# Two graph-attention layers on one core: other places for the mask preparation and the prologue, symmetry check and two normalizations on ScalarE

## The chip, the core and the metric

The kernel runs on one core of a Trainium2 chip. A core has TensorE (matrix products, written as PE), VectorE (DVE), ScalarE (ACT), GpSimd (POOL) and SyncE (SP), which here issues nearly all DMAs. The engines run side by side and wait for each other by semaphores; each works off its own instructions in the order in which the program issues them. The metric is the time of the whole program on the device in microseconds (us), lower is better.

## The reference

x is 16 batches of 1024 rows by 256 features; adj is a symmetric 0/1 matrix of 1024 x 1024 per batch with ones on the diagonal. Two layers are computed, each on relu(layernorm(x)) and each added to x:

```python
h = maximum(layernorm(x), 0)
x = x + L0(h, adj, ...)          # attention with 8 heads of 32, then an MLP
h = maximum(layernorm(x), 0)
x = x + L1(h, adj, ...)          # graph attention with one head

def L0(x, adj):
    qkv = heads(layer_norm(x) * gamma1 + beta1)       # queries = keys = values
    attn = softmax(where(adj > 0, qkv @ qkv.T / sqrt(32), -inf))
    x = x + attn @ qkv
    y = layer_norm(x) * gamma2 + beta2
    return x + gelu(y @ W1 + b1) @ W2 + b2

def L1(f, adj):
    h = f @ W
    e = leaky_relu((h @ a_1).T + h @ a_2 + h @ a_12 @ h.T, 0.2)
    p = softmax(where(adj > 0, e, -9e15))
    return elu(f @ W_1 + (p @ f) @ W_2)
```

## The kernel before

`fast_path` treats the 16 batches in two parts that overlap: while TensorE works on the attention of batch b (`attention`, the first half of the first layer), it also works on what remains of batch b-1 (`rest`: MLP and second layer). A third piece, `prologue`, loads the x of batch b+1 and prepares its h, values va and transposed keys kT meanwhile. Nothing is looped at run time; all instructions are written out.

**The order.** Generators (`stream_a` for the attention, `stream_b` for rest, `stream_p`, `stream_c` for the prologue, `stream_m` for the masks, `stream_k` for the symmetry check, `stream_s`) each hand out a place, a number in which batch b's attention runs from b to b+1. The one with the lowest place issues its next piece. `spread(pieces, n, start, end)` gives n pieces equal distances. So a change of start and end moves a piece's instructions in every queue that it uses. Besides, `defer(us, f)` puts f off until an estimate of the time issued so far, `clock`, has gone on by us; `run_deferred` issues what is due. At the end the program order is fixed for every engine.

**Attention.** A unit is one tile of 128 keys against 512 queries for 4 heads: scores on TensorE (L994), mask added by VectorE (L1007), exponential with row sum by ScalarE (L1014), and one unit later the product with the values (L1109). Batch 0 has 32 units and lets TensorE add half of the masks. From batch 1 on there are 24: since the scores are symmetric, the exponentials of 8 units of the first query half are turned by VectorE (L1030), written to HBM (blocks), and read back for the second half (em, L1077, used by L1091). GpSimd sums up the turned tiles (part, L1043).

**rest.** For four groups c of 256 rows: `prepare` measures mean and variance (`norm_stats`, whose power of -0.5 is on GpSimd, L746) and 5 us later normalizes on VectorE (`normalize`, L750) into y; `turn` transposes y (pty) and applies gamma2 and beta2 (yT); `expand` and `contract` are the MLP (ph, hid, po). `prepare1` and `turn1` do the same for the second layer (ft, ptf, and fT with a relu on ScalarE). Then come the projection uT (copied out of PSUM by ScalarE, L1364), the values gw (by ScalarE and VectorE in turn, L1379), the logits lg with mask and leaky relu on VectorE (L1397, L1402), their exponential (L1403), pf and pa (z and en, L1418 to L1450), and the store. PSUM has three tiles (psm) for all of these but scores and sums.

**prologue.** For four groups: load h, measure, rectify (L803: ScalarE's relu with a scale and a bias nm from VectorE, L798), measure again, values va (L750, L816, L817), transposition ptk and its copy kT (L827). Its 28 pieces lie between b-0.70 and b-0.25.

**Masks.** `turn_masks(b, qh)` loads four row tiles of adj as two halves each (adjp has two buffers), converts them on VectorE to fp8 (mq, L594; `mqp` has one buffer) and turns them by DMA transposes into mk (L904; `mkp` has four). `compare_masks` subtracts, on GpSimd, mk from mq in a block of 128x512 (odd, L919), which is all zeros if adj is symmetric, and VectorE ORs the result into uneven (L926) 3 us later. At the end uneven's largest byte goes into seen, and the program repeats the work on a general path if it isn't 0.

**Buffers.** tmpp holds tags w1 (six buffers: nrm, z, en), w2 (five: os, the copied sums, and ot), y (y and ft) and yT.

```python
            else:
                yield from spread(prologue(b, states[b]), 28, b - 0.700, b - 0.250)
    def stream_m():
        for b in range(B):
            if b:
                yield from spread(turn_masks(b, 0, states[b]), 5, b - 0.17, b - 0.01)
            start = b + (0.36 if b else 0.23)
            yield from spread(turn_masks(b, 1, states[b]), 5, start, start + 0.2)
    def stream_k():
        for b in range(B):
            yield from spread(compare_masks(b, 0, states[b]), TPH, b + 0.02, b + 0.2)
            yield from spread(compare_masks(b, 1, states[b]), 2 * TPH, b + (0.58 if b else 0.52), b + 0.73)
```

Of the kernel before, what the change touches and what calls it, by code (L numbers as in the profile page):

```python
# [9 lines left out]
F32 = mybir.dt.float32  # L10
BF16 = mybir.dt.bfloat16
# [484 lines left out]
def fast_path(  # L496
# [47 lines left out]
    xbp = pool("xbp", NT)  # L544
    adjp = pool("adjp", 2)
    mqp = pool("mqp", 1)
    mkp = pool("mkp", 4)
    hp = pool("hp", 2)
    vp = pool("vp", 2)
    midp = pool("midp", 1)  # L550
# [106 lines left out]

    seen = const.tile([P, 6], F32, name="seen")
    nc.gpsimd.memset(seen[:, 5:6], 0.0)
    uneven = const.tile([P, QW // 2], I32, name="uneven")  # L660
    nc.gpsimd.memset(uneven, 0)

# [70 lines left out]
    def norm_stats(srcs, name):  # L735

        nt = len(srcs)
        st = smallp.tile([P, nt, nc.vector.BN_STATS_DIM], F32, tag="st", name=f"st_{name}")
        mv = smallp.tile([P, nt, nc.vector.BN_AGGR_DIM], F32, tag="mv", name=f"mv_{name}")
        for t in range(nt):  # L740
            nc.vector.bn_stats(st[:, t, :], srcs[t])
            nc.vector.bn_aggr(mv[:, t, :], st[:, t, :])
        ve = smallp.tile([P, nt], F32, tag="ve", name=f"ve_{name}")
        nc.vector.tensor_scalar_add(ve, mv[:, :, 1], EPS)
        rs = smallp.tile([P, nt], F32, tag="rs", name=f"rs_{name}")
        nc.gpsimd.tensor_tensor(rs, ve, mhalf[:, :nt], op=ALU.pow)  # L746
        return mv, rs

    def normalize(dst, src, mv, rs, t):
        nc.vector.tensor_scalar(  # L750
            dst, src, mv[:, t, 0:1], rs[:, t : t + 1], op0=ALU.subtract, op1=ALU.mult
        )

    clock = [0.0]
    deferred = []

    def defer(us, f):
        deferred.append((clock[0] + us, len(deferred), f))  # L760

        return clock[0] + us
# [148 lines left out]
    def compare_masks(b, qh, st):  # L911

        for half in range(qh + 1):
            for i in range(TPH):
                kt = qh * TPH + i
                odd = smallp.tile([P, QW], BF16, tag="odd", bufs=2, name=f"odd_{b}_{qh}_{half}_{i}")
                key = st[half][:, kt // 2, :, kt % 2]
                query = st["mq", qh][:, i, half * QW : (half + 1) * QW]
                nc.gpsimd.tensor_tensor(  # L919
                    odd.rearrange("p (u v x) -> p u v x", u=2, v=2),  # L920
                    key.rearrange("p (u v x) -> p u v x", u=2, v=2),
                    query.rearrange("p (u x v) -> p u v x", u=2, v=2),
                    op=ALU.subtract,
                )
                o = odd.bitcast(I32)
                defer(3.0, lambda o=o: nc.vector.tensor_tensor(uneven, uneven, o, op=ALU.bitwise_or))  # L926
                yield
        if (b, qh) == (B - 1, NQH - 1):
            defer(
                4.0,  # L930
                lambda: nc.vector.tensor_reduce(
                    seen[:, 4:5], uneven.bitcast(U8), axis=mybir.AxisListType.X, op=ALU.max
                ),
            )

# [17 lines left out]
    def finish(b, qh, g, rl, ready, os):  # L953
        h = hs[b]
        run_deferred(ready)
        finished[b, qh] = finished.get((b, qh), 0) + 1
        clock[0] += 0.5
        pt = ps_tile([P, TPH, P], f"ptos_{b}_{g}_{qh}")
        for t in range(TPH):
            nc.tensor.transpose(pt[:, t, :], os[:, t * P : (t + 1) * P], ident)  # L960
        ot = tmpp.tile([P, TPH, GH, HD], F32, tag="w2", bufs=5, name=f"ot_{b}_{g}_{qh}")
        nc.vector.tensor_mul(  # L962
            ot, pt.rearrange("p t (j d) -> p t j d", d=HD), rl.unsqueeze(3).to_broadcast([P, TPH, GH, HD])
        )
        ho = h[qh][:, :, g * P : (g + 1) * P]
        nc.gpsimd.tensor_add(ho, ho, ot.rearrange("p t j d -> p t (j d)"))  # L966

    def attention(b, st):
# [135 lines left out]
        def weigh(qh, g, kt, es, first, last):  # L1104
            if first and not (mirrored and qh == 1):
                acc[g, qh] = pso.tile([P, QW], F32, tag="o", name=f"o_{b}_{g}_{qh}")
            o = acc[g, qh]
            for j in range(GH):
                nc.tensor.matmul(  # L1109
                    o[j * HD : (j + 1) * HD, :],  # L1110
                    va[:, kt, (g * GH + j) * HD : (g * GH + j + 1) * HD],
                    es[j // 2][:, j % 2, :],
                    start=first and not (mirrored and qh == 1),
                    stop=last,
                )
            if last:
                c = os[g, qh] = tmpp.tile([P, QW], F32, tag="w2", bufs=5, name=f"os_{b}_{g}_{qh}")
                nc.vector.tensor_copy(c, o)
                if qh == NQH - 1:
                    close(qh, g)  # L1120
# [89 lines left out]
    def prepare(b, st, c):  # L1210

        h = hs[b]
        assert finished[b, c // 2] == NG
        ts = range(c * TPC, (c + 1) * TPC)
        mv, rs = norm_stats([h[t // TPH][:, t % TPH, :] for t in ts], f"c{b}_{c}")

        def apply():
            y = tmpp.tile([P, TPC, D], F32, tag="y", name=f"y_{b}_{c}")
            for i, t in enumerate(ts):
                normalize(y[:, i, :], h[t // TPH][:, t % TPH, :], mv, rs, i)  # L1220
            st["y", c] = y, None

        st["y", c] = None, defer(5.0, apply)

    def count_fit(lo, hi, i):

# [5 lines left out]
    def rest(b, st, tails):  # L1232
# [30 lines left out]
                yield 0.0, None  # L1263

        def turn(c):
            if st["y", c][1] is not None:
                run_deferred(st["y", c][1])
            y = st["y", c][0]
            for i in range(TPC):
                defer(4.0 * i + 2.0, lambda t=c * TPC + i: add_residuals(t))  # L1270
            yT[c] = tmpp.tile([P, DC, CW], F32, tag="yT", name=f"yT_{b}_{c}")
            pt = ps_tile([P, DC, CW], f"pty_{b}_{c}")
            for dc in range(DC):
                for i in range(TPC):
                    nc.tensor.transpose(
                        pt[:, dc, i * P : (i + 1) * P], y[:, i, dc * P : (dc + 1) * P], ident
                    )
            for dc in range(DC):
                nc.vector.tensor_scalar(  # L1279
                    yT[c][:, dc, :],  # L1280
                    pt[:, dc, :],
                    g2[:, dc : dc + 1],
                    be2[:, dc : dc + 1],
                    op0=ALU.mult,
                    op1=ALU.add,
                )
# [44 lines left out]
        ft, ready1 = {}, {}  # L1331

        def prepare1(c):
            mv, rs = norm_stats(xt[c * TPC : (c + 1) * TPC], f"d{b}_{c}")

            def apply():
                ft[c] = tmpp.tile([P, TPC, D], F32, tag="y", name=f"ft_{b}_{c}")
                for i in range(TPC):
                    normalize(ft[c][:, i, :], xt[c * TPC + i], mv, rs, i)

            ready1[c] = defer(5.0, apply)

        def turn1(c):
            run_deferred(ready1[c])
            fT = st["fT"]
            pt = ps_tile([P, DC, CW], f"ptf_{b}_{c}")
            for i in range(TPC):
                for dc in range(DC):
                    nc.tensor.transpose(
                        pt[:, dc, i * P : (i + 1) * P], ft[c][:, i, dc * P : (dc + 1) * P], ident  # L1350
                    )
            nc.scalar.activation(fT[:, :, c * CW : (c + 1) * CW], pt, AF.Relu)

        def project(qh, oc, fT, uT):
            pp = ps_tile([P, QW], f"puT_{b}_{oc}_{qh}")
# [249 lines left out]
    def stream_c():  # L1605
        for b in range(B):
            if b == 0:
                yield -0.6
                for place, _ in zip((0.02, 0.04, 0.07, 0.10, 0.13), prologue(b, states[b])):
                    yield place  # L1610
            else:
                yield from spread(prologue(b, states[b]), 28, b - 0.700, b - 0.250)

    def stream_m():
        for b in range(B):
            if b:
                yield from spread(turn_masks(b, 0, states[b]), 5, b - 0.17, b - 0.01)
            start = b + (0.36 if b else 0.23)
            yield from spread(turn_masks(b, 1, states[b]), 5, start, start + 0.2)

    def stream_k():
        for b in range(B):
            yield from spread(compare_masks(b, 0, states[b]), TPH, b + 0.02, b + 0.2)
            yield from spread(compare_masks(b, 1, states[b]), 2 * TPH, b + (0.58 if b else 0.52), b + 0.73)

    def stream_s():
        yield -0.3
# [3 lines left out]
        for i, _ in enumerate(check_products()):  # L1631
            yield 1.32 + 0.03 * i

    streams = [stream_s(), stream_a(), stream_b(), stream_p(), stream_c(), stream_m(), stream_k()]
    places = [next(s, None) for s in streams]
    while any(p is not None for p in places):
        i = min((p, i) for i, p in enumerate(places) if p is not None)[1]
# [72 lines left out]
```

## Time and profile before

| | us |
|---|---|
| median of 3 runs | 3430.3 (3427.79 to 3435.07) |
| the profiled execution | 3435.34 |
| its span, first to last instruction | 3433.2 |
| granted TensorE clock in it, share of full speed | 0.993 |

The profile is of one execution. Busy time of an engine is the union of its instructions' times. Batches 2 to 14 take 207 to 215 us each, from the first scores of one to those of the next (the first scores of batch 4 start at 769.4 us, those of batch 5 at 979.5); after 3280 us only the last batch's rest is left. A time named with a position, such as 874.12, counts from the start of the span; the ones named in what follows lie in batch 4's attention or just behind it. A wait is put down to the instruction whose semaphore came last.

The costliest groups (line, engine, operation, output and inputs, shapes, count; busy us, mean ns; idle before):

```profile
L1014 ACT ACTIVATE e<-e 128x512 f32<-128x512 f32 x1504 | 928.5, 619 | 839.7 <-DVE e L1007 837.5
L1007 DVE TENSOR_TENSOR e<-s,mk 128x1024 f32<-128x1024 f32 x752 | 885.1, 1216 | 204.1 <-PE s L994 197.5
```

### The profile page before, as it was taken

Reading aid. Unit: us, or ns where it says so; the run is one execution under the profiler, and the core shown is the slowest. Engines: PE = TensorE matmul, PEld = TensorE weight load, DVE = VectorE, ACT = ScalarE, POOL = GpSimd, SP = SyncE. Lnnn points to the kernel's source line nnn. Section 1 sums busy time; section 2 is a strip of 40 time slices with the busy share of each in tenths; the row PEclk is TensorE's granted clock in tenths of the full one; section 3 lists DMA queues with packets and bytes.
Section 4 is the critical chain, followed back from the end, with each engine's and each line's share of the span. In section 5 each row is a group of like instructions: output and inputs, shape, how many; then the busy total and the mean of one; then the engine's idle time right before and its main releaser. Section 6 shows DMA issues by size and latency. Waiting matters only on the chain. (4 is left out here: it accounts for less than half of the span.)

```text
span 3433.2 us, 114690 instructions
## 1 busy us (share of the span) xinstructions
PE 3239.3 (94%) x48866; PEld 1590.8 (46%) x48866; DVE 2791.5 (81%) x5201; ACT 1966.2 (57%) x4744; POOL 1535.2 (45%) x1758
## 2 busy tenths in 40 slices
PE   6899999999999999999999999999999999999998
PEld 1344444444444444444444444444444444444477
DVE  6788888888888888887888888888888888887844
ACT  6765745647456474655646556475564745646442
POOL 3553553535535254462545526355353554525220
PEclk9999999999999999999999999999999999999999
DMA  5245455464555545555454555545546445554510
GB/s 134 58 115 157 94 121 125 114 158 99 133 121 122 140 109 121 127 120 144 113 134 112 122 138 119 139 109 125 126 113 158 99 121 132 116 143 101 132 38 14
DMA packets 741158, 404.81 MB, mean 118 GB/s; under 512 B 173216, under 2 KB 699936, under 8 KB 740640
## 3 DMA queue, kind: packets, MB, share of 16 engines
q1 hardware_dynamic: 740352, 397.14, 47.9%
q8 instruction: 386, 6.32, 0.8%
q14 instruction: 132, 1.08, 0.1%
q10 hardware_dynamic: 288, 0.26, 0.0%
HBM read 233.97 MB, written 146.54 MB: 111 GB/s over the span
## 5 line engine op out<-in xcount | busy, mean ns | idle before, releaser
L1014 ACT ACTIVATE e<-e 128x512 f32<-128x512 f32 x1504 | 928.5, 619 | 839.7 <-DVE e L1007 837.5
L1007 DVE TENSOR_TENSOR e<-s,mk 128x1024 f32<-128x1024 f32 x752 | 885.1, 1216 | 204.1 <-PE s L994 197.5
L574 PE MATMUL ph<-yT,w 128*32 128x256 f32 x7808 | 445.8, 379 | 16.4 <-DVE yT L1279 15.0
L574 PE MATMUL pa<-gw,e 128*32 128x258 f32 x7584 | 446.4, 380 | 9.1 <-DVE e L1397 9.1
L574 PE MATMUL lg<-fT,uT 128*32 128x256 f32 x7680 | 452.3, 380 | 0.0
L994 PE MATMUL s<-kT 32*64 32x512 f32 x6272 | 447.0, 622 | 1.1 <-DVE e L1007 1.1
L574 PE MATMUL po<-w,hid 128*32 128x256 f32 x7680 | 434.4, 379 | 0.0
L1109 PE MATMUL o<-e,va 128*32 128x512 f32 x3136 | 428.8, 614 | 1.4 <-ACT e L1014 1.4
L574 PEld LDWEIGHTS ph<-yT,w 128*32 128x32 f32 x7808 | 250.4, 110 | 220.2 <-DVE yT L1279 32.5
L574 PEld LDWEIGHTS po<-w,hid 128*32 128x32 f32 x7680 | 250.0, 110 | 202.7 <-issue 48.5
L574 PEld LDWEIGHTS lg<-fT,uT 128*32 128x32 f32 x7680 | 248.5, 110 | 200.2 <-issue 29.7
L574 PEld LDWEIGHTS pa<-gw,e 128*32 128x32 f32 x7584 | 247.5, 110 | 196.0 <-issue 22.1
L1043 POOL TENSOR_TENSOR part<-part,x 128x512 f32<-128x512 f32 x240 | 309.3, 1289 | 18.8
L1030 DVE STREAM_TRANSPOSE x<-e 128x1024 f32<-128x1024 f32 x240 | 291.5, 1232 | 9.9 <-ACT e L1014 8.2
L966 POOL TENSOR_TENSOR h<-h,ot 128x512 f32<-128x512 f32 x64 | 82.1, 1282 | 455.3 <-DVE ot L962 455.3
L1397 DVE SCALAR_TENSOR_TENSOR e<-lg,gw,mk 128x256 f32<-128x256 f32 x512 | 222.9, 476 | 72.3 <-PE lg L574 62.3
L1014 ACT ACTIVATION_READ_ACCUMULATOR e<-e 128x1 f32 x1504 | 281.1, 187 | 0.0
L1403 ACT ACTIVATE e<-e,shift 128x512 f32<-128x512 f32 x256 | 183.1, 716 | 150.8 <-DVE e L1402 141.1
L1303 ACT ACTIVATE hid<-ph,b1c 128x256 f32<-128x256 f32 x512 | 203.6, 465 | 83.7 <-PE ph L574 61.3
L1043 POOL TENSOR_TENSOR part<-x 128x512 f32<-128x512 f32 x120 | 155.3, 1294 | 208.6 <-DVE x L1030 151.2
L919 POOL TENSOR_TENSOR odd<-mk,mq 128x512 bf16<-128x512 fp8e5 x192 | 236.2, 1237 | 20.9 <-DVE uneven L926 18.7
L1109 PEld LDWEIGHTS o<-e,va 128*32 128x32 f32 x3136 | 63.2, 108 | 327.4 <-issue 212.8
(143 smaller groups left out, 4380.4 us busy)
## 6 DMA issues: line engine op xcount, KB each, us to landing
blocks<-x SPq DMA_DIRECT2D x480, 256.0 KB, 4.7
em<-blocks SPq DMA_DIRECT2D x240, 512.0 KB, 5.0
adj<-in_adj_dram SPq DMA_DIRECT2D x248, 256.0 KB, 4.1
h<-in_x_dram SPq DMA_DIRECT2D x64, 256.0 KB, 4.2
xb<-in_x_dram SPq DMA_DIRECT2D x128, 128.0 KB, 3.4
out_dram<-z SPq DMA_DIRECT2D x128, 128.0 KB, 4.1
rows<-row SPq DMA_DIRECT2D x120, 32.0 KB, 2.6
gather<-rows SPq DMA_DIRECT2D x120, 32.0 KB, 3.3
```

Of the source, the lines that this page charges most:

```text
L574: nc.tensor.matmul(out[c : c + HD], lhsT[:, c : c + HD], rhs, start=start, stop=stop)
L919: nc.gpsimd.tensor_tensor(odd.rearrange("p (u v x) -> p u v x", u=2, v=2), key.rearrange("p (u v x) -> p u v x", u=2, v=2), query.rearrang ...
L966: nc.gpsimd.tensor_add(ho, ho, ot.rearrange("p t j d -> p t (j d)"))
L994: nc.tensor.matmul(sc[j // 2][c : c + P // 2, j % 2, :], kT[r, g, kt * P + c : kt * P + c + P // 2], kT[r, g, qs], start=j >= by_pe, stop= ...
L1007: nc.vector.tensor_tensor(e, masked, mb, op=ALU.add)
L1014: nc.scalar.activation(e[:, j], masked[:, j], AF.Exp, scale=SCALE, accum_out=sums[kt // TPH, g][:, n, kt % TPH, qh : qh + 1],)
L1030: nc.vector.transpose(x[:, :, 2 * i : 2 * i + 2, :].rearrange("p c h j -> p h c j"), es[i].rearrange("p h (c i) -> p h c i", i=HD),)
L1043: add = lambda out, p, q: nc.gpsimd.tensor_tensor(out, p, q, op=ALU.add)
L1109: nc.tensor.matmul(o[j * HD : (j + 1) * HD, :], va[:, kt, (g * GH + j) * HD : (g * GH + j + 1) * HD], es[j // 2][:, j % 2, :], start=first ...
L1303: nc.scalar.activation(hid[:, f0 + i, :], ph[:, i, :], AF.Identity, bias=b1c[:, f0 + i : f0 + i + 1])
L1397: nc.vector.scalar_tensor_tensor(e[:, j, :], lg[:, j, :], gw[:, kt, D : D + 1], st[c // 2][:, kt // 2, qs, kt % 2], op0=ALU.add, op1=ALU.add,)
L1403: ready = defer(2.5, lambda: nc.scalar.activation(e, e, AF.Exp, bias=shift))
```

## The change

It has four parts. (1) The prologue's pieces lie between b-0.60 and b-0.15. (2) The masks: turn_masks of the first half goes from b-0.17..b-0.01 to b-0.43..b-0.25 (batch 1: b-0.28..b-0.10), and of the second half, from batch 1 on, from b+0.36..b+0.56 to b+0.03..b+0.20; the comparisons follow each; `mkp` gets a fifth buffer, w2 gives one up. (3) The symmetry check: odd lies in a w1 buffer, and instead of VectorE's OR ScalarE squares it and adds up the row into a column of uneven; at the end the columns are added. (4) y and ft are normalized by ScalarE with a scale and a bias, as the rectify is; the bias nm2 is a small VectorE instruction 3 us after the statistics, and ft's relu is part of it, so that fT is a plain copy.

```diff
-    mkp = pool("mkp", 4)
+    mkp = pool("mkp", 5)
-    uneven = const.tile([P, QW // 2], I32, name="uneven")
-    nc.gpsimd.memset(uneven, 0)
+    uneven = const.tile([P, B * 3 * TPH], F32, name="uneven")
+    def normalize_later(dst, srcs, stats, name, function):
+        mv, rs = stats
+        nm = smallp.tile([P, TPC], F32, tag="nm2", name=f"nm_{name}")
+        defer(
+            3.0, lambda: nc.vector.scalar_tensor_tensor(nm, mv[:, :, 0], -1.0, rs, op0=ALU.mult, op1=ALU.mult)
+        )
+
+        def apply():
+            t = dst()
+            for i, src in enumerate(srcs):
+                nc.scalar.activation(t[:, i, :], src, function, bias=nm[:, i : i + 1], scale=rs[:, i : i + 1])
+
+        return defer(5.0, apply)
...
-                odd = smallp.tile([P, QW], BF16, tag="odd", bufs=2, name=f"odd_{b}_{qh}_{half}_{i}")
+                odd = tmpp.tile([P, QW], BF16, tag="w1", bufs=6, name=f"odd_{b}_{qh}_{half}_{i}")
...
-                o = odd.bitcast(I32)
-                defer(3.0, lambda o=o: nc.vector.tensor_tensor(uneven, uneven, o, op=ALU.bitwise_or))
+                n = (b * 3 + qh + half) * TPH + i
+                defer(
+                    3.0,
+                    lambda odd=odd, n=n: nc.scalar.activation(odd, odd, AF.Square, accum_out=uneven[:, n : n + 1]),
+                )
...
-                    seen[:, 4:5], uneven.bitcast(U8), axis=mybir.AxisListType.X, op=ALU.max
+                    seen[:, 4:5], uneven, axis=mybir.AxisListType.X, op=ALU.add
...
-        ot = tmpp.tile([P, TPH, GH, HD], F32, tag="w2", bufs=5, name=f"ot_{b}_{g}_{qh}")
+        ot = tmpp.tile([P, TPH, GH, HD], F32, tag="w2", bufs=4, name=f"ot_{b}_{g}_{qh}")
...
-        mv, rs = norm_stats([h[t // TPH][:, t % TPH, :] for t in ts], f"c{b}_{c}")
-
-        def apply():
-            y = tmpp.tile([P, TPC, D], F32, tag="y", name=f"y_{b}_{c}")
-            for i, t in enumerate(ts):
-                normalize(y[:, i, :], h[t // TPH][:, t % TPH, :], mv, rs, i)
-            st["y", c] = y, None
-
-        st["y", c] = None, defer(5.0, apply)
+        srcs = [h[t // TPH][:, t % TPH, :] for t in ts]
+
+        def make():
+            y = st["y", c][0] = tmpp.tile([P, TPC, D], F32, tag="y", name=f"y_{b}_{c}")
+            return y
+
+        st["y", c] = [None, normalize_later(make, srcs, norm_stats(srcs, f"c{b}_{c}"), f"c{b}_{c}", AF.Identity)]
...
+            ready1[c] = normalize_later(make, srcs, norm_stats(srcs, f"d{b}_{c}"), f"d{b}_{c}", AF.Relu)
...
-            nc.scalar.activation(fT[:, :, c * CW : (c + 1) * CW], pt, AF.Relu)
+            nc.scalar.copy(fT[:, :, c * CW : (c + 1) * CW], pt)
...
-                yield from spread(prologue(b, states[b]), 28, b - 0.700, b - 0.250)
+                yield from spread(prologue(b, states[b]), 28, b - 0.600, b - 0.150)
...
             if b:
-                yield from spread(turn_masks(b, 0, states[b]), 5, b - 0.17, b - 0.01)
-            start = b + (0.36 if b else 0.23)
-            yield from spread(turn_masks(b, 1, states[b]), 5, start, start + 0.2)
-
-    def stream_k():
-        for b in range(B):
-            yield from spread(compare_masks(b, 0, states[b]), TPH, b + 0.02, b + 0.2)
-            yield from spread(compare_masks(b, 1, states[b]), 2 * TPH, b + (0.58 if b else 0.52), b + 0.73)
+                start, end = (b - 0.28, b - 0.10) if b == 1 else (b - 0.43, b - 0.25)
+                yield from spread(turn_masks(b, 0, states[b]), 5, start, end)
+                yield from spread(compare_masks(b, 0, states[b]), TPH, end + 0.01, end + 0.09)
+                yield from spread(turn_masks(b, 1, states[b]), 5, b + 0.03, b + 0.2)
+                yield from spread(compare_masks(b, 1, states[b]), 2 * TPH, b + 0.21, b + 0.36)
+            else:
+                yield from spread(compare_masks(b, 0, states[b]), TPH, b + 0.02, b + 0.2)
+                yield from spread(turn_masks(b, 1, states[b]), 5, b + 0.23, b + 0.43)
+                yield from spread(compare_masks(b, 1, states[b]), 2 * TPH, b + 0.52, b + 0.7)
```

More of the change, by code (lines that the diff above doesn't have):

```diff
@@ L1116, in weigh @@
             if last:
-                c = os[g, qh] = tmpp.tile([P, QW], F32, tag="w2", bufs=5, name=f"os_{b}_{g}_{qh}")
+                c = os[g, qh] = tmpp.tile([P, QW], F32, tag="w2", bufs=4, name=f"os_{b}_{g}_{qh}")
                 nc.vector.tensor_copy(c, o)
@@ L1265, in turn @@
         def turn(c):
-            if st["y", c][1] is not None:
-                run_deferred(st["y", c][1])
+            run_deferred(st["y", c][1])
             y = st["y", c][0]
@@ L1333, in prepare1, with make @@
         def prepare1(c):
-            mv, rs = norm_stats(xt[c * TPC : (c + 1) * TPC], f"d{b}_{c}")
-            def apply():
+            srcs = xt[c * TPC : (c + 1) * TPC]
+            def make():
                 ft[c] = tmpp.tile([P, TPC, D], F32, tag="y", name=f"ft_{b}_{c}")
-                for i in range(TPC):
-                    normalize(ft[c][:, i, :], xt[c * TPC + i], mv, rs, i)
-            ready1[c] = defer(5.0, apply)
+                return ft[c]
+            ready1[c] = normalize_later(make, srcs, norm_stats(srcs, f"d{b}_{c}"), f"d{b}_{c}", AF.Relu)
         def turn1(c):
@@ L1632, in stream_s @@
             yield 1.32 + 0.03 * i
-    streams = [stream_s(), stream_a(), stream_b(), stream_p(), stream_c(), stream_m(), stream_k()]
+    streams = [stream_s(), stream_a(), stream_b(), stream_p(), stream_c(), stream_m()]
     places = [next(s, None) for s in streams]
```

## The prediction

> **What bounds the kernel now.** The page's first part comes first, then the list of TensorE's waits, then the engines' timelines about one wait.
>
> ```profile
> PE 3239.3 (94%) x48866; PEld 1590.8 (46%) x48866; DVE 2791.5 (81%) x5201; ACT 1966.2 (57%) x4744; POOL 1535.2 (45%) x1758
> ```
>
> TensorE sets the time; 3433.2 - 3239.3 = 194 us is idle, some 22 us of it before the first attention unit. The waits say what the rest is for (us in total, times, longest):
>
> ```profile
> PE ptf L1349 <- ACT uT L1364: 26.1, 14, 1.9
> PE o L1091 <- DMA em<-blocks: 22.9, 19, 2.3
> PE pg L574 <- ACT gw L1379: 20.6, 14, 1.5
> ...
> PE pg L574 <- ACT uT L1364: 18.7, 15, 1.3
> PE ptk L824 <- ACT uT L1364: 18.4, 14, 1.3
> PE ph L574 <- DVE yT L1279: 15.0, 12, 2.0
> PE s L574 <- ACT e L1014: 10.7, 18, 1.4
> PE o L1091 <- DVE os L1118: 10.2, 13, 0.8
> PE pa L574 <- DVE e L1397: 9.1, 14, 0.7
> ```
>
> Four come 14 or 15 times, once a batch, and are PSUM tiles that ScalarE empties late: 26.1 + 20.6 + 18.7 + 18.4 = 83.8 us. TensorE's timeline has two of them, ScalarE's and VectorE's the cause (start, length, engine, line; idle before in brackets):
>
> ```profile
> 871.95 2.22 PE L574 MATMUL pg<-wo,fT 128*32 128x258 f32 x32 [1.48 <-ACT gw L1379]
> 876.04 0.66 PE L1349 MATMUL ptf<-ident,ft 128*128 128x128 f32 x4 [1.86 <-ACT uT L1364]
> ```
> ```profile
> 871.55 0.35 ACT L1379 COPY gw<-pg 128x257 f32<-128x257 f32 x1
> 874.32 1.09 ACT L803 ACTIVATE h<-h,nm,rs_a 128x256 f32<-128x256 f32 x2 [2.42 <-issue]
> 875.32 0.67 ACT L1364 ACTIVATE uT<-puT,w_a 128x512 f32<-128x512 f32 x1
> ```
> ```profile
> 872.96 1.23 DVE L1030 STREAM_TRANSPOSE x<-e 128x1024 f32<-128x1024 f32 x1
> 874.12 0.12 DVE L798 SCALAR_TENSOR_TENSOR nm<-mv_a,rs_a 128x2 f32<-128x2 f32 x1
> ```
>
> ScalarE isn't busy: it stands 2.42 us at the rectify of the next batch (L803), whose factor nm comes at 874.12 from a VectorE deep in its queue, and uT waits behind it. gw was late because the exponentials before it waited for VectorE too.
>
> ```profile
> 864.00:895.00 31.00, 24.71 (x333) 10.07 (x340) 27.95 (x57) 15.74 (x41) 19.38 (x24) 1.00 0.41 97
> 909.00:951.00 42.00, 41.36 (x668) 21.61 (x676) 32.75 (x66) 20.86 (x54) 9.47 (x10) 1.00 0.51 139
> 1020.00:1052.00 32.00, 32.00 (x532) 16.00 (x533) 24.23 (x38) 24.42 (x54) 18.53 (x23) 1.00 0.44 99
> ```
>
> Columns: stretch, its us, busy PE, PEld, DVE, ACT, POOL. In the first, the feature stretch, VectorE is 90% busy and TensorE loses 6.3 us; in the third TensorE loses nothing, but ScalarE is already 76% busy.
>
> **What the skill says.** "TensorE: Matmul & The Clock Gate", section "Architectural detail", calls ScalarE and VectorE strict FIFO; the lines above are just that. Its section "What's actually happening" wants an idle window of about 3.4 us before the clock drops; here 2.20 us did it (at 974.52 eight em matmuls take 1.08 us, elsewhere 0.61, and the next 32 lg 3.15 for 1.91), so the measurement holds: a long em wait costs about 1.7 us more. "Advanced Engine Details and Errata", "Mode Summary", has VectorE's second port shared with GpSimd; y's normalization took 371 to 1443 ns, which agrees. "ScalarE: Activation LUTs", "What ACT_TABLE_LOAD costs", gives 1283 ns; so does the trace.
>
> **The change part by part.** Prices:
>
> ```profile
> L1014 ACT ACTIVATION_READ_ACCUMULATOR e<-e 128x1 f32 x1504 | 281.1, 187 | 0.0
> L926 DVE TENSOR_TENSOR uneven<-uneven,odd 128x256 int32<-128x256 int32 x192 | 142.1, 740 | 33.7 <-POOL odd L919 33.6
> L750 DVE TENSOR_SCALAR y<-h,mv_c,rs_c 128x256 f32<-128x256 f32 x128 | 92.2, 763 | 0.1
> L750 DVE TENSOR_SCALAR ft<-xb,mv_d,rs_d 128x256 f32<-128x256 f32 x128 | 75.5, 631 | 7.2 <-POOL rs_d L746 7.2
> L798 DVE SCALAR_TENSOR_TENSOR nm<-mv_a,rs_a 128x2 f32<-128x2 f32 x64 | 17.1, 267 | 2.5 <-POOL rs_a L746 2.5
> ```
>
> VectorE loses 142.1 + 92.2 + 75.5 = 310 us and gains 128 factors nm2 x 0.27 = 34: 2791 falls to about 2516. ScalarE gains 256 normalizations of 0.55 (L803: two in 1.09) = 140 us, and 192 Squares. No row has a Square; nearest is the 128x512 exponential, which with its read follows the one before in 0.63 us, or alone costs 0.62 + 0.19 = 0.81: 121 to 156 us, I take 125. Its table is unseen: the same page's "Table sets: the hidden batching unit" names relu, copy, identity and abs as fillers of every set, not Square; the trace switches no table for Relu, Identity or Copy. Square is as cheap a function, so I take no load; the other end, two loads a Square, is 192 x 2.57 = 490 us of ScalarE. ScalarE becomes about 2231 us, 65%.
>
> Places: attention unit k of batch b is issued at b + k/25.2 (later 1.15 apart); the second part of b-1 runs at b - 0.01 + us/134. So features begin at 64.8 us, 0.474, and the uT copies are queued at about 0.474, 0.500, 0.566 and 0.579.
>
> (1) Prologue 0.1 later. Steps are 0.0161 apart: rectifies 2 and 3 stood at 0.493 and 0.573, just ahead of uT at 0.500 and 0.579; now 1 and 2 stand at 0.512 and 0.593, just behind. The K transposition after uT (0.589) goes to 0.689. With the mask conversions (0.40 to 0.52, 8 of about 0.5 us) and 4 ft (2.5 us) gone from VectorE about there, its queue is some 3 us shorter, twice the 1.48 us that gw was late. I take four fifths of 83.8: -67 us; bounds -34 and -84. Late next is ft's Relu, which waits for nm2, and that for GpSimd's power.
>
> (2) Masks. The next batch's first half moves from 0.83-0.99 to 0.57-0.75 (batch 1: 0.72-0.90), the second half from 0.36-0.56 to 0.03-0.20. Its adjacency loads and DMA transposes stand in SP's queue before the em loads:
>
> ```profile
> 966.97 1.93 SPq L587 DMA_DIRECT2D adj<-in_adj_dram  x2
> 968.99 1.02 SPq L1077 DMA_DIRECT2D em<-blocks  x2
> ```
>
> adj waits for a conversion on VectorE, em behind it; then TensorE waits 2.20 us at 974.52. The em loads begin at unit 16 (0.635), so the new place meets them as well, but at its beginning, where the first two em loads are already ahead, not at its end. I take half away: -11 us, and -8 for the clock; bounds +10 and -40. The fifth mask buffer makes the early place possible; five masks are alive then. At 0.03-0.20 the second half's 8 loads and 4 DMA transposes stand in SP's queue among mirror writes and xb loads, whose readers come units later, and the prologue's 4 loads of h move with it: 0 each, up to +5 together.
>
> (3) Compares and Squares. The eight of the second half go to 0.21-0.36, the four of the first to 0.76-0.84 of the batch before (batch 0 unmoved). os at unit 16 loses the ORs before it: -7 of 10.2. The 0.65 us of pa at unit 18 stays: conversions replace ORs. In the third stretch ScalarE gets 8 x 0.63 + 2.2 for two pairs of normalizations, less about 1 of rectifying: 24.4 becomes some 31 of 32 us. A Square that is early waits for GpSimd, and behind it hid copies and exponentials, for which TensorE waits. Below nothing it cannot cost, as TensorE is full there; I take 1 us a batch, +15, up to +120. Batch 0 has 12 Squares where ScalarE is 84% busy (41.8 of 50 us, from 50 to 100): +4, bounds 0 and 10.
>
> (4) y and ft themselves: made 5 us before use, hidden by TensorE; in the last batch, without attention, one more hop: +1. Buffers w2 five to four: at most two os and two ot live, 0. Compare tiles in w1: I count four of six live at most, 0, up to +5.
>
> Sum: -67 -11 -8 -7 +15 +4 +1 = -73. From the profiled execution's 3435.3 that is 3362; the median of the runs, 3430.3, is 5 lower: 3357.
>
> **Rivals.** (A) All of it works: 83.8 + 22.9 + 10.2 + 15 = 132, less 12 given back: 3310. For it: VectorE's 276 us; against: em. (B) A wait in place of another: the Relu of ft, waiting for nm2, holds uT as the rectify did, so two fifths of 83.8 go: -34 -6 +15 = -25, 3405. For it: nm2 is due 3 us after the statistics where the old normalization had 5, and GpSimd's part sums run some 6 us in a block (877.4 to 883.3 on its timeline). (C) Slower: ScalarE becomes the bound at 0.21-0.36. A Square is due 3 us after its subtraction; a block of 6 us every two units (15 us) takes 40% of GpSimd's time, so 3.2 of 8 meet one and hold ScalarE some 2.5 us: 8 us a batch, with 1 us free. Held to the full, x 15 = 120 us against the other terms' -88, it gives 3430 + 32 = 3462; with some of its Exp late for o, 3470. It decides from about 5 us of held ScalarE a batch. Against it: at 1019-1038 ScalarE works nearly without pause and TensorE runs on. (D) Squares switch tables: well above 3500. (E) Gains and losses cancel: 3430.
>
> **How the numbers follow.** Main 0.46 (its own range 3330 to 3385), A 0.13, B 0.17, C 0.19, D 0.02, E 0.03. Faster by over 0.2%, about what a measurement of this kernel can tell from no change: 0.46 + 0.13 + 0.17 = 0.76; slower 0.21; between 0.03. The range runs from 3295, below A, to 3445, the lower edge of C.
>
> **What would show it.** Right: the four waits of ScalarE shrink below 20 us together, L803 no longer stands ahead of uT, VectorE near 2520, ScalarE near 2230. The em wait shows near units 17 to 19 or not at all. Wrong: waits of ph or o for hid or e at 0.2 to 0.36 (C), ScalarE waiting for odd, ptf or pg waiting while the Relu of ft waits (B), table loads well over the present 125 (D).

## The result and the profile after

| | before | after |
|---|---|---|
| median of 4 runs, us | 3432.6 | 3398.3 (3397.7 to 3399.1) |
| ratio to before, 95% interval | | 0.990 (0.9885 to 0.9919) |
| profiled execution, us | 3435.3 | 3397.7 |
| its span, us | 3433.2 | 3395.4 |

The change makes the kernel 34 us faster, 1.0%. The direction is as forecast and the time lies within the range, but the gain is less than half of the 73 us that the prediction's main case adds up to. Line numbers of after are a few higher (L1077 of before is L1093, L1091 is L1107, L1364 is L1376). The first part of the page of after:

```profile
PE 3239.8 (95%) x48866; PEld 1600.2 (47%) x48866; DVE 2584.0 (76%) x4881; ACT 2205.2 (65%) x5384; POOL 1515.3 (45%) x1757
```

VectorE is at 2584 us, 207.5 less than before where 276 less were expected, and ScalarE at 2205, 239 more; TensorE's busy time has not changed. Its waits of after, out of the same list:

```profile
PE o L1107 <- DMA em<-blocks: 64.5, 21, 5.2
...
PE o L1107 <- DVE os L1134: 11.0, 12, 1.0
PE pg L574 <- ACT gw L1391: 7.3, 14, 0.5
PE ph L574 <- DVE yT L1292: 7.0, 16, 1.6
PE ptf L1361 <- ACT ft L765: 6.8, 9, 1.3
PE pg L574 <- ACT uT L1376: 6.7, 15, 0.6
```

The four waits of the feature stretch, 83.8 us before, are 7.3 + 6.7 = 14.0, and with the new one for ft's relu 20.8. The wait for em went the other way, from 22.9 to 64.5. Where it sits is seen when the batches are laid over each other. This table is made from the traces: mean us of attention units, batches 3 to 13, from one unit's first score to the next; the last columns are a whole batch, and the time at half the TensorE clock in the whole run, out of the trace's clock records (6.9 to 12.1 us of it lie at the very end of each run).

```
                      units 11-14   16    17    18   23 and 0   batch   half clock
before                       39.2  10.6   9.6  10.4     19.7    210.0     47.9
after                        32.7  10.2  16.6   9.6     17.0    207.2     84.5
e1  masks old                36.8  10.1   9.6   9.5     19.3    206.7     53.1
e2  masks, prologue old      37.9   9.6   9.6   9.5     19.1    206.3     24.1
e3  prologue only            36.9  11.9   9.6   9.5     19.4    208.7     72.9
e4  adj later                33.5  10.1  13.8   9.7     17.0    205.3     45.5
e5  gather later             32.6  10.1  13.9   9.5     17.0    204.3     44.9
e6  both                     33.5  10.1  10.7   9.6     16.9    202.2     23.3
e9  both, where needed       32.8  10.1  10.9   9.6     17.0    201.5     11.8
e10 e9, prologue old         37.7   9.6  10.3   9.5     16.9    204.8     38.7
e11 masks earlier            40.4  10.3   9.6   9.6     17.0    208.2     82.4
```

After gains 6.5 us a batch in the feature stretch, 2.7 at the batch's end and 1.2 at units 16 and 18, and gives 7.0 back at unit 17: 4.6 us of waiting, and 2.4 for a slower clock (5.2 us of the unit are at half speed). TensorE's timeline of after at one unit 17:

```profile
1110.03 1.93 PE L574 MATMUL pa<-gw,e 128*32 128x258 f32 x32
1116.54 1.08 PE L1107 MATMUL o<-em,va 128*32 128x256 f32 x8 [4.58 <-DMA em<-blocks]
```

SP's queue just before it (start and length of the issue, line, output and input, count of DMAs), and the conversion on VectorE:

```profile
1103.30 0.83 SPq L587 DMA_DIRECT2D adj<-in_adj_dram  x2
1104.21 0.38 SPq L1093 DMA_DIRECT2D em<-blocks  x1
1104.65 1.27 SPq L917 DMA_TRANSPOSE mk<-mq  x1
1108.40 0.81 SPq L587 DMA_DIRECT2D adj<-in_adj_dram  x2
1109.26 2.49 SPq L1084 DMA_DIRECT2D gather<-rows  x4
1111.85 1.51 SPq L1093 DMA_DIRECT2D em<-blocks  x2
```
```profile
1107.95 0.76 DVE L594 TENSOR_SCALAR mq<-adj 128x512 fp8e5<-128x512 int32 x2
```

The em load that is issued at 1111.85 could have gone at about 1105.9, after the transpose: the product that frees its buffer had ended at 1105.1. First the adjacency load waits for its buffers until the conversion of 1107.95 has begun to free them, then four loads of the row sums (gather, which unit 17 asks for) take 2.49 us to issue. The em load lands 4.7 us after its issue, and TensorE waits from 1111.96 to 1116.54. Windows of after show what follows, and that ScalarE isn't the cause (stretch, us, busy PE, PEld, DVE, ACT, POOL, then the granted clock):

```profile
1009.00:1041.00 32.00, 32.00 (x533) 15.66 (x532) 20.87 (x29) 28.40 (x68) 26.37 (x30) 1.00 0.44 87
1105.00:1122.00 17.00, 12.42 (x160) 5.74 (x156) 9.56 (x23) 5.65 (x14) 5.05 (x8) 0.80 0.87 211
```

In the first, where the Squares are, ScalarE works 89% of the time and TensorE without a gap. In the second, at unit 17, the clock is granted at 0.80. The DMA engines are 87% busy there, so slow transfers could be the cause too; the two theories below stand for that.

### The profile page after: what moved, and what is told of

It is laid out like the page before. It is cut to its first block, busy times and chain, and to the rows that moved or that the text cites. A ratio compares the mean times of both kernels' runs of the same rounds, so it can differ in the third digit from the quotient of the medians.

```text
span 3395.4 us, 114970 instructions
## 1 busy us (share of the span) xinstructions
PE 3239.8 (95%) x48866; PEld 1600.2 (47%) x48866; DVE 2584.0 (76%) x4881; ACT 2205.2 (65%) x5384; POOL 1515.3 (45%) x1757
## 5 line engine op out<-in xcount | busy, mean ns | idle before, releaser
L574 PE MATMUL lg<-fT,uT 128*32 128x256 f32 x7680 | 471.1, 392 | 0.0
L574 PEld LDWEIGHTS lg<-fT,uT 128*32 128x32 f32 x7680 | 255.8, 113 | 211.0 <-issue 48.4
L829 POOL TENSOR_TENSOR nrm<-nrm,g 128x256 f32<-128x256 f32 x128 | 110.8, 865 | 312.3 <-DVE nrm L749 312.3
L745 POOL TENSOR_TENSOR rs_c<-ve_c,mhalf 128x2 f32<-128x2 f32 x64 | 44.7, 699 | 421.0 <-DVE ve_c L743 421.0
L932 POOL TENSOR_TENSOR odd<-mk,mq 128x512 bf16<-128x512 fp8e5 x192 | 220.8, 1165 | 25.2 <-DMA mk<-mq 25.2
```

The source lines that it names most:

```text
L574: nc.tensor.matmul(out[c : c + HD], lhsT[:, c : c + HD], rhs, start=start, stop=stop)
L932: nc.gpsimd.tensor_tensor(odd.rearrange("p (u v x) -> p u v x", u=2, v=2), key.rearrange("p (u v x) -> p u v x", u=2, v=2), query.rearrang ...
```

## The experiments

Two theories of the em wait stood against each other: Q, the order in SP's queue (the load is issued late), and T, the traffic of the mask loads and transposes (the load is slow once issued). Two more stood for the feature waits: O, the order of rectify and uT in ScalarE's queue, and R, the relief of VectorE as a whole.

**e1: masks and comparisons at their old places**, the rest as changed.

```diff
-                start, end = (b - 0.28, b - 0.10) if b == 1 else (b - 0.43, b - 0.25)
-                yield from spread(turn_masks(b, 0, states[b]), 5, start, end)
+                yield from spread(turn_masks(b, 0, states[b]), 5, b - 0.17, b - 0.01)
...
+    def stream_k():
```

> The changed kernel with the masks and comparisons at their old places; prologue, Squares and normalizations stay as changed. Theory Q (SP's order: at unit 17 adjacency loads that wait for a conversion, and the gather, stand ahead of an em load; about 7 us a batch, 98 us in all): unit 17 goes back from 16.6 to about 9.6 us, a smaller em wait returns at unit 23 (23 to 45 us in all), some conversions return to the feature stretch (0 to 25 us): 3330 to 3360. Theory T (traffic: the transposes and adjacency loads slow the em loads wherever they meet): the wait only moves to unit 23, 3385 to 3410.

3387.1 us, ratio 0.9865 (0.9849 to 0.9882). By number that is outside Q's range and inside T's. By place it speaks for Q: unit 17 is back at 9.6 us, and the em wait, now at the batch's end, is 21.9 us; had the 64.5 us only moved there, as T has it, they would stand there. The number is high for another reason: units 11 to 14 lose 4.1 us a batch with the conversions back, more than I had allowed:

```profile
PE ptf L1361 <- DVE xb L1340: 26.6, 7, 5.0
PE pg L574 <- ACT uT L1376: 22.7, 15, 1.8
PE o L1107 <- DMA em<-blocks: 21.9, 19, 2.2
```

So the move of the masks wins about 4.1 + 2.3 us a batch and loses 7.0.

**e2: only the engines changed**; masks old as in e1, and prologue old too.

```diff
-                yield from spread(prologue(b, states[b]), 28, b - 0.600, b - 0.150)
+                yield from spread(prologue(b, states[b]), 28, b - 0.700, b - 0.250)
```

> Masks and prologue at their old places; only Squares, normalizations on ScalarE and the buffers are changed. If the order of rectify and uT in ScalarE's queue makes the waits of the feature stretch (theory O): 3415 to 3435. If the relief of VectorE makes them go (theory R): 3360 to 3390.

3386.2 us, ratio 0.9865 (0.9848 to 0.9881): R's number, but not R's reason. The waits for uT stand as before:

```profile
PE ptf L1361 <- ACT uT L1376: 25.4, 14, 1.8
...
PE ptk L837 <- ACT uT L1376: 18.4, 14, 1.3
```

The gain lies at units 16 and 18, which wait for os and pa no more (1.9 us a batch), and in small parts elsewhere; the clock is at half for 24.1 us in place of 47.9.

**e3: only the prologue moved**, in the kernel before.

```diff
-                yield from spread(prologue(b, states[b]), 28, b - 0.700, b - 0.250)
+                yield from spread(prologue(b, states[b]), 28, b - 0.600, b - 0.150)
```

> The kernel before with the prologue alone 0.1 later. Theory O: most of 63 us of the feature waits go, 3375 to 3395. Theory R: 3415 to 3435.

3413.9 us, ratio 0.9938 (0.9922 to 0.9955), between the two. The waits of ptf and ptk for uT are gone, as O has it; those of pg for gw (16.1 us) and for uT (15.9) stay. Two others grew, out of TensorE's waits in e3:

```profile
PE o L1091 <- DVE os L1118: 30.4, 14, 2.3
PE ptf L1349 <- DVE xb L1327: 27.3, 7, 5.1
...
PE pg L574 <- ACT gw L1379: 16.1, 12, 2.0
PE pg L574 <- ACT uT L1364: 15.9, 15, 1.7
```

The first was 10.2 us before; of the second, the list of before has

```profile
PE ptf L1349 <- DVE xb L1327: 4.7, 14, 1.0
```

VectorE, still with its conversions, ORs and normalizations, is late in other places. Between e2 and e1, where the prologue's place is the only difference, it is alike: ptf and ptk stop waiting for uT, ptf waits 26.6 us for xb, and the time changes by under 1 us.

**e4: each adjacency load after the first 4 us later**, so that SP comes to it when its buffer is free; amount and place of the traffic stay.

```diff
+        def fetch_later(i):
+            due[0] = defer(4.0, lambda: raw.append(fetch_mask(b, ts[i])))
...
-        raw = fetch_mask(b, ts[1])
+        fetch_later(1)
...
-                raw = fetch_mask(b, ts[i + 2])
+                fetch_later(i + 2)
```

> The changed kernel, each adjacency load after the first put off by 4 us of the clock, so that the conversion which frees its buffers is done when SP comes to it; amount and places of the traffic stay. Theory Q: SP is held some 3 us less ahead of the em load of unit 17, which with the clock is 3 to 5 us a batch: 3330 to 3355. Theory T: 3390 to 3405.

3378.0 us, ratio 0.9836 (0.9820 to 0.9853). That lies between the two ranges, 23 us above Q's and 12 below T's. Unit 17 falls from 16.6 to 13.8 us, a little less than Q has it. Batch 0 takes 127.3 us in place of 119.8, which takes 7.5 us of the gain back.

**e5: the gather one unit later.**

```diff
-            if n == NG * NT + 1:
+            if n == NG * NT + 2:
                 gather(1)
```

> The changed kernel with the four gather loads of the second head group issued at unit 18 and not at 17; adjacency loads as changed. Theory Q: SP is free for the em load some 2.5 us sooner, the wait of 4.6 us at unit 17 becomes about 2 and the clock drops less often: 3340 to 3365. Theory T (traffic): 3390 to 3405.

3354.8 us, ratio 0.9770 (0.9750 to 0.9790): within Q's range. Four small loads that TensorE doesn't wait for cost 44 us where they stood. The em wait:

```profile
PE o L1107 <- DMA em<-blocks: 40.0, 23, 2.8
```

**e6: both**, the loads put off from batch 1 on.

> Both: gather at unit 18, and from batch 1 on each adjacency load put off by 4 us. Theory Q: nothing is left ahead of the em load, unit 17 goes back to about 9.6 us, 7 us less a batch: 3295 to 3320. Theory T: 3370 or more.

3337.6 us, ratio 0.9724 (0.9703 to 0.9746). That is 18 us above Q's range and 32 below T's. Q's 7 us a batch are 5.9 here (16.6 to 10.7), and batch 0 takes 127.2 us again.

Whether the load comes late or is slow can be read from the traces as well. This table is of the fourth em load of a batch, for which unit 17 waits longest (means of batches 3 to 13; the issue counts from the first score of unit 16):

```
        issued at, us   issue to landing, us
before           11.3                    4.6
after            16.8                    5.0
e4               15.2                    5.0
e5               14.7                    5.4
e6               11.6                    6.4
e9               11.6                    6.5
```

In after the load is issued 5.5 us later than before and takes only 0.4 longer. In e6 it is issued as early as before, and then takes 1.8 longer. So the wait of 4.6 us is Q's, and T has its part in what is left.

**e7 and e8: Squares alone, and normalizations alone**, each in the kernel before (e8 with four w2 buffers for room).

> The kernel before with the Squares on ScalarE alone (odd keeps its own two buffers). The ORs stood at units 14 to 18, ahead of the os copy and of the masks of pa: units 16 and 18 lose about 2 us a batch, 3400 to 3412. If it is VectorE's load as a whole that counts, 142 of the 310 us that left it: about 3412 too, but with the gain spread over all units. If ScalarE suffers from waiting for GpSimd: 3430 or more.

> The kernel before with y and ft normalized on ScalarE alone (w2 with four buffers, for room). If the gain of 47 us of both together sits in units 16 and 18 (Squares), this gives 3415 to 3432; if in the feature stretch and in the clock, 3395 to 3412.

e7: 3418.6 us, ratio 0.9960 (0.9943 to 0.9976); e8: 3416.8, ratio 0.9955 (0.9938 to 0.9972). Each wins some 13 us: e8 is in its first range, e7 is 7 us above the range that it had for units 16 and 18. The Squares do it at units 16 and 18 as expected (9.6 and 9.5 us), though batch 0 takes 123.6 us with them in place of 118.9. Together they won 47: the two aren't additive. Part of the rest is seen in the traces: with both, batch 0 takes 118.5 us (e8 120.2), and the clock is at half for 24.1 us, where each alone has 56.2 (e7) and 46.9 (e8). Why the clock drops less often with both was not tested.

**e9: as e6, but the adjacency loads put off only where they meet em loads** (first halves of batches 2 to 15).

```diff
+        def fetch_later(i):
+            if qh or b < 2:
+                raw.append(fetch_mask(b, ts[i]))
+            else:
                 due[0] = defer(4.0, lambda: raw.append(fetch_mask(b, ts[i])))
...
-            if n == NG * NT + 1:
+            if n == NG * NT + 2:
                 gather(1)
```

> As e6, but the adjacency loads are put off only for the first half of batches 2 to 15, the ones that meet the em loads. Batch 0, which lost 7 us in e6, goes back to about 120 us, and the ptf wait of 1.1 us a batch at unit 11 goes back to 0.35: 3315 to 3333. If putting the loads off isn't what cost batch 0: 3337.

3316.8 us, ratio 0.9665 (0.9647 to 0.9682), in its range, the fastest of all and 2.4% below the changed kernel. Batch 0 is at 121.1. Its page, its em wait, and SP's queue and TensorE at a unit 17:

```profile
PE 3212.8 (97%) x48866; PEld 1591.5 (48%) x48866; DVE 2593.6 (78%) x4881; ACT 2201.8 (66%) x5384; POOL 1518.7 (46%) x1757
```
```profile
PE o L1116 <- DMA em<-blocks: 14.1, 15, 1.7
```
```profile
1081.73 0.38 SPq L1102 DMA_DIRECT2D em<-blocks  x1
1082.17 1.26 SPq L925 DMA_TRANSPOSE mk<-mq  x1
1083.48 0.57 SPq L1102 DMA_DIRECT2D em<-blocks  x1
1085.93 0.82 SPq L587 DMA_DIRECT2D adj<-in_adj_dram  x2
```
```profile
1090.67 0.64 PE L1116 MATMUL o<-em,va 128*32 128x256 f32 x8 [1.18 <-DMA em<-blocks]
```

The em load of 1083.48 stands right behind the transpose now. It still takes until 1090.67, some 7 us, with a transpose and adjacency loads beside it: about 1 us a batch of waiting is left, and by the table above that part is a slower transfer, as T has it. Which of the transfers beside it slows it was not tested.

**e10: e9 with the prologue at its old place.**

> e9 with the prologue at its old place, so that rectifies 2 and 3 stand ahead of uT again. Theory O (order in ScalarE's queue): pg, ptf and ptk wait 4 to 6 us more a batch, 55 to 90 us: 3375 to 3420. Theory R (VectorE's relief alone is enough once the conversions are gone from there): 3320 to 3345.

3370.2 us, ratio 0.9823 (0.9804 to 0.9842), 53 us slower than e9: 5 us under O's range and 25 above R's. Three of the four waits of before are back; that of pg for gw is not (8.6 us, in e9 7.3):

```profile
PE ptf L1370 <- ACT uT L1385: 24.3, 14, 1.8
PE pg L574 <- ACT uT L1385: 18.6, 15, 1.3
...
PE ptk L837 <- ACT uT L1385: 10.6, 14, 1.1
```

O holds for the waits for uT, once the conversions are out of the way: R isn't enough by itself.

**e11: the first half's masks ahead of all em loads**, in the feature stretch.

```diff
-                start, end = (b - 0.28, b - 0.10) if b == 1 else (b - 0.43, b - 0.25)
+                start, end = (b - 0.28, b - 0.10) if b == 1 else (b - 0.64, b - 0.46)
```

> The changed kernel with the first half's masks at 0.36 to 0.54 of the batch before, ahead of all em loads but in the feature stretch. Theory Q: no em wait (-7 us a batch), but the conversions bring back about 4 us a batch of feature waits, as in e1: 3345 to 3365. Were the em wait due to the masks' traffic or the fifth buffer alone: 3390 or more.

3415.3 us, ratio 0.9954 (0.9937 to 0.9971): Q's number is missed by 50. Unit 17 is at 9.6 and no em wait is left, as Q has it, so that the time above 3390 doesn't speak for traffic or for the fifth buffer; but units 11 to 14 take 40.4 us. TensorE's largest wait of e11, then SP's queue and VectorE's timeline at one unit 10:

```profile
PE ptf L1361 <- ACT ft L765: 50.4, 13, 4.4
```
```profile
1251.03 4.05 SPq L1053 DMA_DIRECT2D blocks<-x  x4
1255.13 7.82 SPq L587 DMA_DIRECT2D adj<-in_adj_dram  x4
```
```profile
1260.47 0.43 DVE L594 TENSOR_SCALAR mq<-adj 128x512 fp8e5<-128x512 int32 x1 [2.85 <-DMA adj<-in_adj_dram]
1262.17 0.43 DVE L594 TENSOR_SCALAR mq<-adj 128x512 fp8e5<-128x512 int32 x1 [1.27 <-DMA adj<-in_adj_dram]
```

The adjacency loads stand behind the writes of the turned tiles, and VectorE, with the next scores' masks behind the conversion, waits 4.1 us for them. It is the same fault one queue further, as far as these lines show: what is late in SP's order holds VectorE, that holds the factor of ft, and that TensorE.

## Why the prediction came out as it did

**What bounds the kernel, and the feature stretch (1).** Right in mechanism; by its own four waits right in size as well: 67 us expected, 63 measured net (83.8 less 20.8). By units the stretch gave more, 6.5 us a batch or some 90 us in all. ptf no longer waits for xb (4.7 us before), and all eight clock drops that before has in these units are gone (27 us at half speed); the working put both at nothing. It also gave nearly the whole to the prologue's place, with VectorE's relief as help. The runs show that it takes both: the place alone won 20 (e3) or nothing (e2 to e1), the relief alone left the uT waits standing (e2), and with both done e10 prices the place at 53 us. The relief itself was smaller than priced. One reason is the small factors, priced at the 267 ns of L798 before:

```profile
L759 DVE SCALAR_TENSOR_TENSOR nm_d<-mv_d,rs_d 128x2 f32<-128x2 f32 x64 | 38.4, 600 | 26.8 <-POOL rs_d L745 26.7
L811 DVE SCALAR_TENSOR_TENSOR nm<-mv_a,rs_a 128x2 f32<-128x2 f32 x64 | 34.5, 540 | 2.5 <-POOL rs_a L745 2.5
```

Out of the trace: where no GpSimd instruction ran beside it, nm_d took 156 ns in the mean, and where one did (31 of 64) 1073. Of the 64 nm of the prologue, 46 have GpSimd beside them now, 16 had it before.

**Masks (2): the step that failed.** It read SP's queue right and saw that adj waits for a conversion and em behind it, and that the new place meets the em loads. Then it took half of the wait away, because at the beginning of the em loads "the first two em loads are already ahead": -11 us, and -8 for the clock. Measured is +41.6 us of waiting; at unit 17 with the clock 7.0 us a batch, of which 2.7 come back at the batch's end. The third and fourth em loads come just there, and the working missed what else SP has to issue at unit 17: the four gather loads, 2.49 us, which before stood among em loads alone. e5 and e4 show both terms, 44 and 20 us, and e6 and e9 that with both gone the shift of the masks pays. The upper bound of +10 was too narrow for the same reason.

**Squares and ScalarE (3).** The price was right: a Square took 0.62 us and 0.19 for the read, and there are no further table loads (62 + 46 + 15 + 1 + 1 = 125 as before). So Square behaved here like the cheap functions that "ScalarE: Activation LUTs", section "Table sets: the hidden batching unit", has in every set, though it isn't named there. The +15 us for waits behind ScalarE was wrong: it stood 66.9 us behind GpSimd's odd in the whole run, and TensorE has no wait for hid or e in those units. Rival C named a real hold and over-priced its effect. os at unit 16 kept its wait (11.0 us), where -7 was expected. The ORs had been its cause, as unit 16 is at 9.6 without them (e2, e7), but the prologue at its new place brings a wait of its own (10.1 in e1, 11.9 in e3; 10.1 in e9 against 9.6 in e10). pa at unit 18, expected to stay, lost its 9.1. Batch 0 took 0.9 us more (+4 expected; 4.7 with the Squares alone).

**y and ft (4).** Two waits for y, 3.3 us together, came in, and the last batch with its tail went from 353.5 to 352.0 us: nothing to speak of.

**The sum.** By units it is -6.5 +7.0 -2.7 -1.2 and +0.6 elsewhere, -2.8 us a batch. That the time lies in the range is in part luck: two errors met. In e9 the em wait is 14.1 us, about the half of before's 22.9 that step (2) expected, and e9 takes 3316.8 us, 40 less than the forecast of 3357. So the other steps gave more than they were priced at, mostly in the feature stretch, and step (2) took more than that back. Rival B has nearly the measured time, but not its reason: the relu of ft held TensorE 6.8 us in after, and 50 only in e11.

## What to carry to other kernels

A queue that only issues DMAs can be in the critical path like an engine: when a step moves, list every issue that will stand between a free buffer and the load that fills it, those of small loads and of other parts too, with their issue times and with what each waits for. A load that must wait for a compute engine belongs behind the loads that needn't, or later by the time it would wait. When a wait goes, look at the unit where the moved work now lies, by laying the periods over each other, before believing the sum.

## What was unexpected of the hardware

ScalarE at 89% busy over 32 us cost TensorE nothing, although in the whole run it also waited 66.9 us for GpSimd. What covers this, the three PSUM tiles or the unit between exponential and product, was not tested.

The clock costs more than the waits show. In the changed kernel a drop lasts 3.4 us at half speed in the trace's clock records, or twice that; it has 16 of them, 14 at unit 17 of a batch and the last one, longer, at the run's end. e9 has 2. The idle window of about 3.4 us that "TensorE: Matmul & The Clock Gate", section "What's actually happening", wants is not what these traces show: in the kernel before a wait of 2.20 us was followed by a drop. Within a run the drops start on a grid of 3.41 us, and they follow TensorE's busy share in the grid window just before. Counted over all 13 traces, from batch 1 on to the last score, windows at full clock: of 66 in which TensorE was busy for under 40%, all were followed by a drop; of 66 with 40 to 48%, 37; of 132 with 48 to 60%, 3; of 11283 with more, none. So several short waits close together can do it as well: in before, the eight drops at units 12 and 13 each follow waits of 1.5 and 1.9 us.
